# Conditioned attention on one core: another order of the Strassen products, new tables of PSUM banks, and an end in halves and pairs of heads

## The chip, the core and the metric

The kernel runs on one core of a Trainium2 chip. The time is the device time of one execution in microseconds (us); times of before and after are medians of several runs. TensorE does the matrix products and writes them to PSUM, which has eight banks of 128 x 512 f32. ScalarE (ACT in the profile), VectorE (DVE) read the banks; GpSimd (POOL) works in SBUF only here; SyncE (SP) issues most DMAs. All arithmetic but that of the row maxima's split is f32.

## The reference

Attention with 16 heads of 32 over 8 sequences of 512 tokens, with a condition added to Q and K and the input added at the end:

```python
Q = _split_heads(x @ Wq.T + bq)
K = _split_heads(x @ Wk.T + bk)
V = _split_heads(x @ Wv.T + bv)
tQ = _split_heads(tokens @ Wq.T + bq)
tK = _split_heads(tokens @ Wk.T + bk)
cQ = Q + tQ
cK = K + tK
scores = jnp.einsum('bhqd,bhkd->bhqk', cQ, cK) / jnp.sqrt(jnp.float32(HEAD_DIM))
attn = jax.nn.softmax(scores, axis=-1)
out = jnp.einsum('bhqk,bhkd->bhqd', attn, V)
return x + out.transpose(0, 2, 1, 3).reshape(B, S, D_MODEL)
```

Here x is (8, 512, 512), tokens are (8, 1, 512), the weights 512 x 512.

## The kernel before, in words

The work is cut into 32 tiles t: sequence b = t // 4 and group r = t % 4 of four heads. A group's four heads lie on the four blocks of 32 partitions, so four products with a depth of 32 run at the same time on TensorE.

**A stage.** The loop over t has four stages, one for each block kc of 128 keys. Each begins with `exponentials(t, kc)`: for each head, the transposed row maximum is put in its bank by a product with ones (L485), the transposed scores are added to it (L488), and ScalarE takes the exponential into SBUF (L500 and, for two banks at once, L502). Then `row_max` of a later tile computes scores for 128 queries (L417); VectorE takes the negated maximum of two banks at a time (L426), and `denominators` has ScalarE compute the exponentials once more, into a tile that nobody reads, for their sums (L443). What follows depends on the stage:

- first stage: x is transposed for a later sequence (L225), and Q of a later tile pair is projected;
- second: `weighted` multiplies the exponentials with V (L507), copied out by VectorE (L529);
- third: K is projected; in odd t also `output` of the tile before, which transposes (L539), divides (L553), adds the input (L564, POOL) and stores;
- fourth: `transpose_max` turns the maxima of the next tile (L469, copied by L475), and V is projected (L320); in even t `output` stands here.

`split_max` (L457 to L460, POOL) divides a maximum into three bf16 parts before its transposes.

**Projections.** A sequence's projection is made by Strassen-like block products, seven products M1 to M7 in place of eight, of 256 columns each; block sums of x and of the weights (`xc`, `wc`) are prepared by VectorE and POOL. `project_pair` does one pair of head groups in two parts. `first_products` (odd t for Q and K, even t for V) makes M1, M6, M7 and half of M2's depth; ScalarE copies M1 out (L359), and VectorE adds the rest (L368, L346 or L343, L371 or L365). `other_products` makes M4, M5, the other half of M2, and M3, and adds them in (L382, L383, L346). Each product with its two depth blocks is four passes on TensorE. Tiles of the first sequence are projected by plain products instead (L255 and L281).

**Order.** The order on TensorE, ScalarE, VectorE and POOL is the order of the program; nothing is moved by a scheduler. Waits come from the data and from PSUM. All PSUM is one tile of eight banks, and `TURNS` says for each stage which banks serve: places 0 to 3 are the banks of the exponentials (2 and 3 next to each other), which serve other work once they are read, and 4 to 7 those of the scores for the maxima. A bank can be written again when its last reader is done. Eight tables are used in turn in the loop, from the fourth on in the prologue, and five more near the end.

**The end.** From t = 28 on there is less to project. The weighted sums are made in two halves there (`first_half`, L693, and `second_half`, L699), and the maxima of the last tile in pairs of heads by `row_max_pair`. In the last tile no denominators are computed beforehand: the exponentials are summed (`acc`, L823 and L827) and multiplied by ones (L517).

Of the kernel before, what the change touches and what calls it, by code (L numbers as in the profile page):

```python
# [9 lines left out]
F32 = mybir.dt.float32  # L10
BF16 = mybir.dt.bfloat16
AF = mybir.ActivationFunctionType
ALU = mybir.AluOpType
# [4 lines left out]
def kernel(  # L18
# [33 lines left out]
    nc = tc.nc  # L52
# [26 lines left out]
        (0, 3, 6, 7, 1, 2, 4, 5),  # L79
        (7, 2, 0, 1, 3, 4, 5, 6),  # L80
        (0, 3, 1, 2, 4, 5, 6, 7),
        (2, 3, 4, 5, 6, 7, 0, 1),
        (7, 2, 5, 6, 0, 1, 3, 4),
        (5, 2, 0, 1, 3, 4, 6, 7),
        (2, 3, 0, 1, 4, 5, 6, 7),
        (0, 5, 3, 4, 6, 7, 1, 2),

        (2, 5, 6, 7, 0, 1, 3, 4),
        (2, 5, 0, 1, 3, 4, 6, 7),
        (2, 5, 3, 4, 6, 7, 0, 1),  # L90
        (2, 5, 6, 7, 0, 1, 3, 4),
        (2, 5, 0, 1, 3, 4, 6, 7),
# [221 lines left out]
    def product(n, b, u, i, pt, kcs=(0, 1)):  # L314

        for kc in kcs:
            w = block_of_w(n, i, u, kc)
            if n == "v":
                xb = block_of_x(b, i, kc, slice(u * P, (u + 1) * P))
                nc.tensor.matmul(pt, xb, w, start=(kc == kcs[0]), stop=(kc == kcs[-1]))  # L320
            else:
                xb = block_of_x(b, i, kc, slice(0, HS))
                nc.tensor.matmul(pt, w, xb, start=(kc == kcs[0]), stop=(kc == kcs[-1]))  # L323
# [24 lines left out]
    def first_products(n, b, u, dens, small, late):  # L348

        one_, two_ = (banks(1), banks(2)) if late else (banks(0), banks(3))
        c1, c12, c2, c22 = parts_of(n, b, u)
        m1 = c2[:, 0, :]
        product(n, b, u, 1, one_[:, :HS])
        if late:
            product(n, b, u, 2, one_[:, HS:], (0,))
        nc.scalar.copy(m1, one_[:, :HS])  # L359
        dens()  # L360
        small()
        product(n, b, u, 6, two_[:, :HS])
        product(n, b, u, 7, two_[:, HS:])
        if late:
            nc.vector.tensor_tensor(c1[:, 0, :], one_[:, HS:], m1, ALU.add)  # L365
        else:
            product(n, b, u, 2, one_[:, HS:], (0,))
        nc.vector.tensor_tensor(c12, two_[:, :HS], m1, ALU.add)  # L368
        plus(n, b, u, 1, c22, two_[:, HS:], c12)
        if not late:  # L370
            nc.vector.tensor_tensor(c1[:, 0, :], one_[:, HS:], m1, ALU.add)  # L371

    def other_products(n, b, u, dens, small, at):
# [5 lines left out]
        product(n, b, u, 2, two_[:, :HS], (1,))  # L379
# [26 lines left out]
    def row_max(t, qc):  # L406
        if t >= T:
            return
        open_max(t)
        for j in range(HG):  # L410
            row_scores(t, qc, j, banks(HG + j))
        for pr in range(NP):
            row_max_of(t, qc, pr, banks(HG + pr * 2, 2))
# [16 lines left out]
    def row_max_pair(t, qc, pr):  # L430

        open_max(t)
        for i in range(2):
            row_scores(t, qc, pr * 2 + i, banks(2 + i))
        row_max_of(t, qc, pr, banks(2, 2))
# [28 lines left out]
    def transpose_max(t, bank):  # L464
# [10 lines left out]
        nc.vector.tensor_copy(maxT[t], pt[:, :S])  # L475
# [84 lines left out]
    def finish(t):  # L560
        b, g = divmod(t, G)
        y = res.pop(t)
        last = nc.vector if t == T - 1 else nc.gpsimd
# [91 lines left out]
    project_qk(1, "q", banks(0))  # L655
# [15 lines left out]
    transpose_x(NS + 2, banks(2))  # L671
    project_qk(2, "k", banks(1))
# [4 lines left out]
    transpose_x(NS + 3, banks(0))  # L677
    project_qk(3, "q", banks(2))
# [28 lines left out]
    for t in range(T - 3):  # L707
# [6 lines left out]
        if r % 2:  # L714
            turn_x = lambda: transpose_x(t + NS + 3, banks(1), nc.vector.tensor_copy)
            project_pair("q", *qk_of, dens, turn_x, False)
        else:
            transpose_x(t + NS + 3, banks(0), nc.scalar.copy)
            if t:
                project_pair("q", *qk_of, dens, nothing, (1, 2))  # L720
            else:
                dens()
                project_qk(3, "k", banks(1))
# [18 lines left out]
        if r % 2:  # L742
            project_pair("k", *qk_of, dens, lambda: output(t - 1, banks(1)), False)
        elif t:
            project_pair("k", *qk_of, dens, nothing, (0, 2))
        else:
            dens()
            project_v(3, banks(2))
# [5 lines left out]
        denominators(t + 2, 0, [0])  # L754
        transpose_max(t + 1, banks(0))
        rest = lambda: denominators(t + 2, 0, [1])
        put_out = lambda: output(t - 1, banks(3)) if t else None
        if r % 2:
            project_pair("v", b + 1, r, rest, nothing, (1, 3))
        else:  # L760
            project_pair("v", b + 1, r, rest, put_out, True)
        if t == T - 4:
            first_half(t, banks(1))
# [27 lines left out]
    row_max(t + 2, 2)  # L791
    transpose_max(t + 1, banks(0))
    row_max_pair(t + 2, 1, 1)
# [6 lines left out]
    row_max(t + 1, 3)  # L800
    split_max(t + 1)
    second_half(t - 1, pd)

    exponentials(t, 1, (3, 4, 6, 7))
    times_v(t, 0, pv)
    output(t - 1, pd)
    exponentials(t, 2, (0, 1, 3, 4))
    times_v(t, 1, pv)
    transpose_max(t + 1, pd)
    exponentials(t, 3, (6, 7, 0, 1))  # L810
    times_v(t, 2, pv)
    exponentials(t + 1, 0, (3, 4, 6, 7))
# [3 lines left out]
    output(t, pd)  # L816
    t += 1
    exponentials(t, 1, (0, 1, 3, 4))
# [5 lines left out]
    exponentials(t, 2, (6, 7, 0, 1))  # L824
# [3 lines left out]
    exponentials(t, 3, (3, 4, 6, 7))  # L828
# [3 lines left out]
    times_v(t, 3, pv)  # L832
    den = stage.tile([P, NC, D], F32, tag="w", name="den")[:, 0, :]
    nc.scalar.copy(den, pd)
    leave(t, pv)
    untranspose(den, psum[:, 0, :])
    untranspose(oT[t], psum[:, 1, :])
    invert(t, psum[:, 0, :].rearrange("p (c h e) -> p c h e", c=NS, h=HG)[:, :, :, 0:1])
    divide(t, psum[:, 1, :])
    finish(t)  # L840
# [31 lines left out]
```

## Time and profile before

| what | us |
|---|---|
| median of 3 runs | 775.22 (773.84 to 775.51) |
| the profiled execution | 773.71 |
| its span in the profile | 771.9 |
| TensorE busy | 756.5 |
| ScalarE busy | 626.2 |
| VectorE busy | 528.7 |
| POOL busy | 124.5 |
| first L485 of t = 0 | 58.38 after the start |
| first L485 of t = 30 | 739.71 after the start |

A row of the timeline has the start, the time from the first to the last end of the instructions merged in it, the engine, the line, the operation, its tiles and shapes and, in brackets, the idle time before it and what ended that. An f32 product is two records, one for each pass. The ends of TensorE's records are modelled: a record of 256 columns shows 0.38 us while the next one starts much sooner, so the starts of successive rows say more than the busy time.

### The profile page before, as it was taken

To read this page: it belongs to the slowest core of one execution; us is meant where nothing else is said; L and a number is where in the kernel's file an instruction comes from. 1 tells how busy PE (TensorE), PEld (TensorE's weight loads), DVE (VectorE), ACT (ScalarE), POOL (GpSimd) and SP (SyncE) were. 2 spreads that over 40 slices of the span, in tenths; PEclk is the share of its full clock that TensorE was granted. 3 is DMA by queue.
4 is the path that set the end of the run, shared out by engine and by line. 5 is a ranking of instruction groups with operands and counts; after the bars stand their busy time and mean duration, and the time that the engine had idled before them with its cause. 6 is when DMAs were issued, how large, how long until landed. Compare 5 with 4: busy or idle time off the path is not lost.

```text
span 771.9 us, 14075 instructions
## 1 busy us (share of the span) xinstructions
PE 756.5 (98%) x5368; PEld 427.8 (55%) x5368; DVE 528.7 (68%) x719; ACT 626.2 (81%) x1452; POOL 124.5 (16%) x209
## 2 busy tenths in 40 slices
PE   8999999999999999999999999999999999999896
PEld 5443566555556655556655555665555565555332
DVE  4455677677677776677767776777766777667754
ACT  2447788888888888888888888888888888888864
POOL 0062011111011111111111101111110111110120
PEclk9999999999999999999999999999999999999999
DMA  9010011101111110111111011110101101010100
GB/s 314 17 39 28 14 42 42 28 16 42 42 42 42 32 40 15 42 42 42 42 25 45 14 43 42 42 42 12 45 2 28 29 28 29 1 44 12 48 22 28
DMA packets 41555, 29.76 MB, mean 39 GB/s; under 512 B 2824, under 2 KB 35592, under 8 KB 41488
## 3 DMA queue, kind: packets, MB, share of 16 engines
q1 hardware_dynamic: 40912, 27.81, 12.5%
q10 hardware_dynamic: 576, 1.05, 0.4%
q8 instruction: 42, 0.69, 0.4%
q14 instruction: 25, 0.20, 0.1%
HBM read 20.47 MB, written 8.39 MB: 37 GB/s over the span
## 4 chain that ended last, share of the span: by engine, by line
PE 95%; DVE 2%; ACT 1%; DMA 1%; issue 0%; SPq 0%; DVEq 0%; ACTq 0%
PE psum L323 23%; PE psum L507 15%; PE psum L488 14%; PE psum L417 14%; PE psum L320 12%; PE psum L485 6%; PE psum L255 4%; PE psum L225 2%; PE psum L539 2%; PE psum L281 2%; PE psum L469 1%; ACT e L500 1%; DVE nmax L426 1%; DMA x<-in_x_dram 1%; PE psum L180 1%; ACT e L502 0%
## 5 line engine op out<-in xcount | busy, mean ns | idle before, releaser
L426 DVE TENSOR_REDUCE nmax<-psum 128x2 f32<-128x1024 f32 x256 | 301.7, 1219 | 146.6 <-PE psum L417 145.8
L443 ACT ACTIVATE dead<-psum,nmax 128x512 f32<-128x512 f32 x496 | 335.1, 691 | 26.9 <-DVE nmax L426 26.9
L500 ACT ACTIVATE e<-psum 128x512 f32<-128x512 f32 x270 | 145.8, 595 | 88.8 <-PE psum L488 88.8
L417 PE MATMUL psum<-kT,qT 32*128 32x512 f32 x1024 | 140.9, 598 | 0.9 <-ACT e L502 0.9
L488 PE MATMUL psum<-qT,kT 32*128 32x512 f32 x1024 | 132.7, 588 | 0.0
L502 ACT ACTIVATE e<-psum 128x1024 f32<-128x1024 f32 x121 | 124.9, 1032 | 0.0
L507 PE MATMUL psum<-e,v 128*32 128x512 f32 x1024 | 118.6, 596 | 0.1
L443 ACT ACTIVATION_READ_ACCUMULATOR dead<-psum,nmax 128x1 f32 x496 | 103.6, 209 | 0.0
L457 POOL CAST split<-nmax 128x16 bf16<-128x16 f32 x32 | 8.1, 254 | 551.4 <-DVE nmax L426 551.4
L417 PEld LDWEIGHTS psum<-kT,qT 32*128 32x128 f32 x1024 | 67.5, 183 | 51.7 <-ACT dead L443 31.1
L507 PEld LDWEIGHTS psum<-e,v 128*32 128x32 f32 x1024 | 29.5, 109 | 82.4 <-issue 58.6
L485 PE MATMUL psum<-maxT,onesb 3*128 3x512 bf16 x512 | 51.8, 384 | 2.1 <-DVE res L553 0.8
L488 PEld LDWEIGHTS psum<-qT,kT 32*128 32x128 f32 x1024 | 51.1, 185 | 2.5
L564 POOL TENSOR_TENSOR res<-res,xr 128x512 f32<-128x512 f32 x31 | 39.4, 1272 | 74.0 <-DVE res L553 74.0
L485 PEld LDWEIGHTS <-onesb 3*128 3x128 bf16 x512 | 13.4, 91 | 64.8 <-issue 60.0
L529 DVE COPY oT<-psum 128x512 f32<-128x512 f32 x30 | 20.8, 692 | 39.7 <-PE psum L507 39.7
L323 PE MATMUL psum<-xc,wc_q 128*128 128x256 f32 x168 | 41.1, 380 | 0.2
L323 PE MATMUL psum<-xc,wc_k 128*128 128x256 f32 x168 | 40.9, 379 | 0.0
L320 PE MATMUL psum<-wc_v,xc 128*128 128x256 f32 x168 | 40.9, 379 | 0.0
L129 POOL TENSOR_TENSOR xr<-xr,bvb 128x512 f32<-128x512 f32 x32 | 40.5, 1268 | 0.0
L323 PEld LDWEIGHTS psum<-xc,wc_q 128*128 128x128 f32 x168 | 30.8, 190 | 4.6 <-ACT e L502 1.0
L320 PEld LDWEIGHTS psum<-wc_v,xc 128*128 128x128 f32 x168 | 30.9, 190 | 3.7
(135 smaller groups left out, 817.5 us busy)
## 6 DMA issues: line engine op xcount, KB each, us to landing
x<-in_x_dram SPq DMA_DIRECT2D x33, 256.0 KB, 2.7
xr<-in_x_dram SPq DMA_DIRECT2D x32, 256.0 KB, 3.1
out_dram<-res SPq DMA_DIRECT2D x32, 256.0 KB, 2.4
w_q<-in_L_cond_Wq_dram ACTq DMA_DIRECT2D x4, 256.0 KB, 4.4
w_k<-in_L_cond_Wk_dram SPq DMA_DIRECT2D x4, 256.0 KB, 5.0
w_v<-in_L_cond_Wv_dram SPq DMA_DIRECT2D x4, 256.0 KB, 6.0
bvb<-in_L_cond_bv_dram SPq DMA_DIRECT2D x1, 256.0 KB, 5.3
cond_sb<-in_cond_dram SPq DMA_DIRECT2D x1, 16.0 KB
```

The source lines that it names most:

```text
L129: nc.gpsimd.tensor_tensor(xr[t], xr[t], bias, ALU.add)
L320: nc.tensor.matmul(pt, xb, w, start=(kc == kcs[0]), stop=(kc == kcs[-1]))
L323: nc.tensor.matmul(pt, w, xb, start=(kc == kcs[0]), stop=(kc == kcs[-1]))
L417: nc.tensor.matmul(pt, qkT["q", t][r, qc * P : (qc + 1) * P], qkT["k", t][r, :], start=True, stop=True,)
L426: nc.vector.tensor_reduce(nmax[t][:, qc, pr * 2 : pr * 2 + 2, 0], pt, AX.X, ALU.max, negate=True)
L443: nc.scalar.activation(dead, banks(HG + j), AF.Exp, bias=nmax[t][:, qc, j, :], accum_out=sums[t][:, qc, j, :],)
L485: nc.tensor.matmul(bank[j], onesb[r, :], maxT[t][r, :], start=True, stop=False)
L488: nc.tensor.matmul(bank[j], qkT["k", t][r, kc * P : (kc + 1) * P], qkT["q", t][r, :], start=False, stop=True,)
L500: nc.scalar.activation(e[:, i, :], bank[pr * 2 + i], AF.Exp)
L502: nc.scalar.activation(e, banks(2, 2), AF.Exp)
L507: nc.tensor.matmul(pt[j * HD : (j + 1) * HD, :], vs[b % 2][:, kc, (g * HG + j) * HD : (g * HG + j + 1) * HD], es[t, kc, j // 2][:, j % 2, ...
L564: last.tensor_tensor(y, y, xr.pop(t), ALU.add)
```

## The change

1. `first_products` puts M6 and the half of M2 in one bank and M7, which now comes last, in the second half of M1's bank, for Q, K and V alike. `late` and its two forms are gone.
2. V's first half has all of M1 before the transposes of the maximum and, in even t, of the output; V's other half has M4 and M5 before the transposes (`small` is now called in `other_products` too). All four denominators stand behind the copy of M1, where two stood ahead.
3. Of K's M2, the half depth of the first part is made for 128 of the 256 columns. For the others POOL copies M1, and `other_products` makes both depth blocks.
4. New tables of banks, and other places in them for the work of the prologue and the loop.
5. In the fourth stage of t = 28 ScalarE copies the transposed maxima, the denominators come after that, and the output uses another bank.
6. The maxima of the last tile are spread over other stages in pairs of heads (`row_max_pairs`); t = 30 has its output behind the next exponentials, with the addition by VectorE; the last tile's output is copied, divided, added and stored in two halves.

```diff
     TURNS = [
-        (0, 3, 6, 7, 1, 2, 4, 5),
         (7, 2, 0, 1, 3, 4, 5, 6),
-        (0, 3, 1, 2, 4, 5, 6, 7),
-        (2, 3, 4, 5, 6, 7, 0, 1),
-        (7, 2, 5, 6, 0, 1, 3, 4),
-        (5, 2, 0, 1, 3, 4, 6, 7),
-        (2, 3, 0, 1, 4, 5, 6, 7),
-        (0, 5, 3, 4, 6, 7, 1, 2),
-
-        (2, 5, 6, 7, 0, 1, 3, 4),
-        (2, 5, 0, 1, 3, 4, 6, 7),
+        (7, 0, 3, 4, 5, 6, 1, 2),
+        (3, 0, 4, 5, 1, 2, 6, 7),
+        (2, 5, 0, 1, 6, 7, 3, 4),
+        (7, 0, 5, 6, 3, 4, 1, 2),
+        (3, 0, 4, 5, 1, 2, 6, 7),
+        (4, 5, 0, 1, 6, 7, 2, 3),
+        (5, 0, 6, 7, 1, 2, 3, 4),
+
+        (2, 5, 6, 7, 3, 4, 0, 1),
+        (2, 5, 3, 4, 0, 1, 6, 7),
+        (2, 5, 0, 1, 6, 7, 3, 4),
+        (2, 5, 6, 7, 3, 4, 0, 1),
         (2, 5, 3, 4, 6, 7, 0, 1),
-        (2, 5, 6, 7, 0, 1, 3, 4),
-        (2, 5, 0, 1, 3, 4, 6, 7),
     ]
...
-    def first_products(n, b, u, dens, small, late):
-        one_, two_ = (banks(1), banks(2)) if late else (banks(0), banks(3))
+    def first_products(n, b, u, dens, small, at):
+        one_, two_ = banks(0), banks(at)
         c1, c12, c2, c22 = parts_of(n, b, u)
         m1 = c2[:, 0, :]
         product(n, b, u, 1, one_[:, :HS])
-        if late:
-            product(n, b, u, 2, one_[:, HS:], (0,))
         nc.scalar.copy(m1, one_[:, :HS])
         dens()
         small()
         product(n, b, u, 6, two_[:, :HS])
-        product(n, b, u, 7, two_[:, HS:])
-        if late:
-            nc.vector.tensor_tensor(c1[:, 0, :], one_[:, HS:], m1, ALU.add)
-        else:
-            product(n, b, u, 2, one_[:, HS:], (0,))
+        w = P if n == "k" else HS
+        product(n, b, u, 2, two_[:, HS : HS + w], (0,), slice(0, w))
+        product(n, b, u, 7, one_[:, HS:])
         nc.vector.tensor_tensor(c12, two_[:, :HS], m1, ALU.add)
-        plus(n, b, u, 1, c22, two_[:, HS:], c12)
-        if not late:
-            nc.vector.tensor_tensor(c1[:, 0, :], one_[:, HS:], m1, ALU.add)
+        nc.vector.tensor_tensor(c1[:, 0, :w], two_[:, HS : HS + w], m1[:, :w], ALU.add)
+        if w < HS:
+            nc.gpsimd.tensor_copy(c1[:, 0, w:], m1[:, w:])
+        plus(n, b, u, 1, c22, one_[:, HS:], c12)
...
         product(n, b, u, 4, one_[:, :HS])
         product(n, b, u, 5, one_[:, HS:])
-        product(n, b, u, 2, two_[:, :HS], (1,))
+        small()
+        if n == "k":
+            product(n, b, u, 2, two_[:, :P], (1,), slice(0, P))
+            product(n, b, u, 2, two_[:, P:HS], (1, 0), slice(P, HS))
+        else:
+            product(n, b, u, 2, two_[:, :HS], (1,))
         product(n, b, u, 3, two_[:, HS:])
...
+    def row_max_pairs(t, of, late=()):
+        open_max(t)
+        for k, (qc, pr) in enumerate(of):
+            for i in range(2):
+                row_scores(t, qc, pr * 2 + i, banks(HG + k * 2 + i))
+        row_max_of(t, *of[0], banks(HG, 2))
+        for f in late:
+            f()
+        row_max_of(t, *of[1], banks(HG + 2, 2))
...
-            project_v(3, banks(2))
+            project_v(3, banks(0))
...
         row_max(t + 2, 0)
-        denominators(t + 2, 0, [0])
-        transpose_max(t + 1, banks(0))
-        rest = lambda: denominators(t + 2, 0, [1])
-        put_out = lambda: output(t - 1, banks(3)) if t else None
-        if r % 2:
-            project_pair("v", b + 1, r, rest, nothing, (1, 3))
-        else:
-            project_pair("v", b + 1, r, rest, put_out, True)
         if t == T - 4:
-            first_half(t, banks(1))
+            transpose_max(t + 1, banks(0), nc.scalar.copy)
+            denominators(t + 2, 0)
+            output(t - 1, banks(1))
+            first_half(t, banks(3))
+            break
+        dens = lambda: denominators(t + 2, 0)
+
+        def small():
+            transpose_max(t + 1, banks(1))
+            if t and r % 2 == 0:
+                output(t - 1, banks(2))
+
+        project_pair("v", b + 1, r, dens, small, (0, 2) if r % 2 else 3)
         advance()
...
     exponentials(t, 3)
-    row_max(t + 2, 2)
-    transpose_max(t + 1, banks(0))
-    row_max_pair(t + 2, 1, 1)
+    row_max_pairs(
+        t + 2, [(1, 1), (2, 0)], [lambda: transpose_max(t + 1, banks(0))]
+    )
...
     exponentials(t, 0)
-    row_max(t + 1, 3)
+    row_max_pairs(t + 1, [(2, 1), (3, 0)])
+    second_half(t - 1, pd)
+
+    exponentials(t, 1, (3, 4, 6, 7))
+    row_max_pair(t + 1, 3, 1, HG + 2)
     split_max(t + 1)
-    second_half(t - 1, pd)
-
-    exponentials(t, 1, (3, 4, 6, 7))
     times_v(t, 0, pv)
...
     invert(t, sums[t])
-    output(t, pd)
     t += 1
-    exponentials(t, 1, (0, 1, 3, 4))
+    exponentials(t, 1, (3, 4, 0, 1))
+    untranspose(oT[t - 1], pd)
+    divide(t - 1, pd)
     times_v(t, 0, pv)
...
     nc.scalar.copy(den, pd)
-    leave(t, pv)
-    untranspose(den, psum[:, 0, :])
-    untranspose(oT[t], psum[:, 1, :])
-    invert(t, psum[:, 0, :].rearrange("p (c h e) -> p c h e", c=NS, h=HG)[:, :, :, 0:1])
-    divide(t, psum[:, 1, :])
-    finish(t)
+    oT[t] = op.tile([P, S], F32, tag="oT", name=f"oT_{t}")
+    two = [slice(0, HS), slice(HS, S)]
+    nc.vector.tensor_copy(oT[t][:, two[0]], pv[:, two[0]])
+    nc.scalar.copy(oT[t][:, two[1]], pv[:, two[1]])
+    pi, po = psum[:, 3, :], [psum[:, 4, :], psum[:, 6, :]]
+    untranspose(den, pi)
...
+    for i in range(2):
+        cs = slice(i * 2, i * 2 + 2)
+        for qc in (i * 2, i * 2 + 1):
+            nc.tensor.transpose(
+                po[i][:, qc * P : (qc + 1) * P], oT[t][:, qc * P : (qc + 1) * P], ident
+            )
...
+        last = (nc.gpsimd, nc.vector)[i]
+        last.tensor_tensor(res[t][:, cs], res[t][:, cs], xr[t][:, cs], ALU.add)
+        (nc.sync, nc.scalar)[i].dma_start(
+            out[b].rearrange("(c p) d -> p c d", p=P)[:, cs, g * P : (g + 1) * P], res[t][:, cs]
+        )
```

## The prediction

> **What bounds the kernel now.** I read the page first (busy shares, clock, chain), then TensorE's timeline in the steady loop, in the first tile and at the end, then VectorE's timeline beside it. All names and lines are those of the kernel before; a "stage" runs from one L485 row to the next.
>
> ```profile
> PE 756.5 (98%) x5368; PEld 427.8 (55%) x5368; DVE 528.7 (68%) x719; ACT 626.2 (81%) x1452; POOL 124.5 (16%) x209
> ...
> PEclk9999999999999999999999999999999999999999
> ...
> PE 95%; DVE 2%; ACT 1%; DMA 1%; issue 0%; SPq 0%; DVEq 0%; ACTq 0%
> ```
>
> TensorE is busy for 98% at full clock and is 95% of the chain. No other engine's average can give time back; only TensorE's own work, and the short holes inside its "busy" rows, can. These show in the starts of successive rows:
>
> ```profile
> 277.85 1.02 PE L417 MATMUL psum<-kT,qT 32*128 32x512 f32 x8
> 278.81 1.13 PE L323 MATMUL psum<-xT,wT_k 128*128 128x256 f32 x4
> ...
> 283.55 1.11 PE L417 MATMUL psum<-kT,qT 32*128 32x512 f32 x8
> 284.59 0.40 PE L469 MATMUL psum<-identb,split 128*128 128x128 bf16 x4
> 284.88 1.13 PE L320 MATMUL psum<-wT_v,xc 128*128 128x256 f32 x4
> 285.85 1.03 PE L320 MATMUL psum<-wc_v,xc 128*128 128x256 f32 x4
> 286.72 0.59 PE L320 MATMUL psum<-wT_v,xT 128*128 128x256 f32 x2
> ```
>
> A record is one pass. Passes of 256 columns follow each other every 0.216 us (285.85 to 286.72: four in 0.87), four concurrent 512-column ones every 0.43. Two fixed costs stand out. A change between the 32-row groups and the full array costs 0.095 (277.85 to 278.81 is 0.96 for 0.86 of work), and the first full f32 pass after it 0.104 more (284.88 to 285.85 is 0.97 for 0.86). Those remain. Beyond them are waits: 283.55 to 284.59 is 1.04, 0.08 over the 0.96; and the four transposes of the maximum take 0.29 instead of 0.22, after which the product pays its 0.104. The eight stages of the pair t=9, 10 start at 265.31, 271.06, 276.76, 282.47, 288.11, 293.76, 299.38, 304.64 and the next pair at 310.73; this repeats to 0.01 us through the loop.
>
> ```profile
> 270.81 0.42 DVE L368 TENSOR_TENSOR qT<-psum,qT 128x256 f32<-128x256 f32 x1 [0.36 <-PE psum L323]
> 271.27 0.48 DVE L346 SCALAR_TENSOR_TENSOR qT<-psum,tok,qT 128x256 f32<-128x256 f32 x1
> 271.67 0.41 DVE L371 TENSOR_TENSOR qT<-psum,qT 128x256 f32<-128x256 f32 x1
> ```
>
> This is where the 0.08 comes from: three additions end a first half, and the last ends at 272.08, 1.02 into the next stage. Its bank is L417's fourth, due at 1.09, and the weight load before it needs 0.1.
>
> ```profile
> 54.18 0.39 PE L469 MATMUL psum<-identb,split 128*128 128x128 bf16 x4
> 54.40 0.60 PE L225 MATMUL psum<-ident,x 128*128 128x128 f32 x4
> 54.84 3.60 PE L255 MATMUL psum<-xT,wT_q 128*128 128x512 f32 x8
> ...
> 59.29 0.39 PE L485 MATMUL psum<-maxT,onesb 3*128 3x512 bf16 x3 [0.53 <-DVE qT L268]
> ...
> 74.37 3.70 PE L281 MATMUL psum<-wT_v,xT 128*128 128x512 f32 x8 [1.22 <-ACT e L502]
> ...
> 716.58 0.66 PE L539 MATMUL psum<-ident,oT 128*128 128x128 f32 x4 [0.80 <-ACT e L502]
> ...
> 739.71 0.40 PE L485 MATMUL psum<-maxT,onesb 3*128 3x512 bf16 x4 [0.54 <-DVE maxT L475]
> ...
> 755.05 0.66 PE L539 MATMUL psum<-ident,oT 128*128 128x128 f32 x4 [0.87 <-DVE oT L529]
> ...
> 768.64 0.37 SPq L565 DMA_DIRECT2D out_dram<-res  x1
> ```
>
> These are the waits that come once: two in tile 0, three at the end, and the last store.
>
> **The loop, stage by stage** (odd t does first halves, even t the others).
>
> *M6 and M2 in one bank, M7 last.* The first two additions now run during M7's 0.86 us and one remains: it should end about 0.7 into the next stage, not 1.02. In the new tables its bank is L417's fourth or an earlier finished one. So the stage after Q's first half falls from 5.70 to the 5.62 of its even twin (293.76 to 299.38): 14 x 0.08 = 1.1. The Q stage itself begins behind V's first half in the same way (266.40 to 267.40, 0.05 too long): 12 x 0.05 = 0.6; at t=25 and 27, with no x left to transpose, M6 waits for the pair of exponentials at 3.34 in both kernels.
>
> *A quarter of K's M2 moved.* 0.216 leaves each odd third stage and enters each even one: zero on TensorE, whose columns are the same. But four passes of 256 columns become eight of 128. The row: f32 transposes of 128 columns, each with its own weight load, come every 0.109 (54.40 to 54.84), and the load of an f32 product shows as 0.104 where nothing covers it, so it just fits under 0.109. The Trainium skill ("TensorE: Matmul & The Clock Gate", section "Back-to-back issue gap") speaks against the split: in a stream of loads and matmuls it has some 81 ns each at 128 columns where streaming alone would need 56, because the load has its own budget. By the row the split costs nothing; with the page's 25 ns on 8 passes x 14 pairs, an estimate of 2.8 us. Bounds: zero (no column is saved, so no gain) to the load wholly bare, 8 x 0.104 x 14 = 11.6. I take zero, by the nearer row. The longer even stage also takes off a wait: its last denominators (ending at 305.58 in the trace, 0.94 into the next) now land before L417. VectorE's addition shrinks to 128 columns. POOL gets a copy of 128 columns, between the 0.25 of a 16-column cast and the 1.27 of a 512-column addition. It queues behind split and the output's addition and delays the residual's bias by that much, read stages later; its own reader comes four stages later. POOL is 16% busy: zero, and at most its own length if that cover were gone.
>
> *V's halves begin with products.* In odd t the transposes of the maximum move behind M4 and M5. At 54.18 such transposes inside full-array work cost 0.22 with no restart; I add 0.05 for the f32 load that four 0.056 passes cannot cover. The stage becomes 2.04 (to the end of L417 and the change) + 0.97 + 0.86 + 0.27 + 0.43 + 0.86 + 0.10 = 5.54 instead of 5.64: 14 x 0.10 = 1.4. maxT is then copied at about 4.9, 0.6 before its use. In even t M1 comes first, then the transposes, ready at 3.24, then the output's transposes. These now go to the third exponential bank, which the pair releases at 3.34 (716.58 is 3.34 after its stage's start). So 3.34 + 0.49 + 2.26 = 6.09, and L417's wait for K's last addition (0.02 more) gives 6.11 against 6.08: 13 x 0.03 = 0.4 lost. What is late there is no longer L417 but the pair. Bounds for the moved transposes: at best 0.05 better in odd t, where the f32 load is covered after all; at worst both restarts come again in the middle, +0.2 on 27 stages. I stay near 54.18, the only row of the kind.
>
> **Tile 0.** L485 of its first stage no longer uses the bank of L268: 0.7, and 0.2 in the two holes behind it, so 6.98 becomes 6.07. project_v(3) goes to the first exponential bank, free at its turn: the 1.3 before 74.37. In the fourth stage M6 waits for the pair: +0.05. Together 2.1. A new wait, of the first burst's fourth bank on a weight transpose that ScalarE ends at 24.4, is hidden: TensorE waits there for ScalarE at 29.3 anyway.
>
> **The end.** *t=28, fourth stage*: the output's transposes use the second bank (free at 2.42), and the pair's wait then starts first_half at 3.34: 5.19 instead of 5.78, 0.59. ScalarE's copy of maxT (0.47 by the spacing after its x copy) makes its denominators late and costs the next L417 0.23. *t=29, fourth stage*: maxT follows one maximum instead of two and two score tiles leave: 4.99 becomes 3.86, 1.13; the score pair comes back at t=30, second stage, as 0.95 less an 0.3 wait and rounding: 0.57. *t=30's output behind t=31's exponentials*: the 0.87 and its restart go; L485's second half then waits 0.2 for ScalarE: 0.6. The sums acc follow ScalarE, 0.1 sooner. *Halves*: den and its transposes as before; VectorE's half copy (0.41), ScalarE's after it (same bank, 0.37), then divide and add by halves, the POOL one about 0.7. The last store starts near 768.05 of the old scale instead of 768.64: 0.6. The addition and store of t=30 move from POOL to VectorE, behind acc; SP gets them about 5 us later than today (757.88), still 5 before the end. Two queues carry the last 128 KB each; I give the transfer no gain. Together 0.36 + 0.56 + 0.6 + 0.1 + 0.6 = 2.2.
>
> **Sum.** 1.1 + 0.6 + 1.4 - 0.4 + 2.1 + 2.2 = 7.0, and 0.1 of rounding: 7.1 us. The profiled execution took 773.71 (span 771.9, 1.8 around it), so it would take 766.6; it lies 1.5 under the median of the three runs, 775.22. The forecast is made on the median: 775.2 - 7.1 = 768.1.
>
> **Rivals.**
> - *The split M2 is bound by weight loads (slower).* Place: eight 128-column passes of 14 K pairs. Price: up to 0.104 each, 11.6, so 775.2 - 7.1 + 11.6 = 779.7. It turns the sign above 7.1 / 112 = 63 ns a pass. For it: 0.104 against 0.109 is no margin. Against: the transposes keep 0.109.
> - *The transposes restart the array.* Moved into the middle they pay 0.095 and 0.104 again: 27 x 0.2 = 5.4 back, 773.5. For it: behind L469 today the 0.104 is paid. Against: 54.18.
> - *The waits only change their name.* L417 still waits for the last addition (1.7 lost) and the even fourth stage pays another restart behind the pair (1.3): 771.1. For it: the addition's margin is 0.3 only.
>
> **How the numbers follow.** Forecast 0.72, its own range 766.0 to 770.5; names changed 0.10; restart 0.11; loads 0.07. The range, 765.0 to 772.0, takes in the third rival and leaves out 0.18. This measurement can tell about 0.2%, 1.55 us. Faster: 0.72 + 0.10 + half of the restart = 0.88. Same: the other half, 0.05. Slower: 0.07.
>
> **What will show it.** Right: stages of an odd/even pair near 5.71, 5.62, 5.49, 5.54, 5.66, 5.62, 5.48, 6.11; no hole before 59.29 and 74.37; two final stores on two queues. Wrong: 128-column passes more than 0.11 apart; a product's first pass behind L469 at 0.32; L417 rows over 1.05; an even fourth stage over 6.15.

## The result, and the profile after

| what | before | after |
|---|---|---|
| median, us | 774.41 (773.63 to 775.51, 6 runs) | 768.11 (766.91 to 770.46, 6 runs) |
| ratio | | 0.9922 [0.9905, 0.9939] |
| the profiled execution | 773.71 | 767.80 |
| its span | 771.9 | 766.0 |

The changed kernel is 0.8% faster. The forecast of 768.1 was a gain of 7.1 from a median of 775.2; with more runs the median of before is 774.4, and the two medians lie 6.3 apart. That 768.1 and 768.11 agree so closely is luck: the base was 0.8 too high and the gain 0.8 too large. In the two profiles, counted from the first exponentials, the loop and the end take 713.55 and 707.59, a gain of 5.96. The stages of the loop that the prediction listed came out within 0.03 us of it; what is missing of 7.1 in this profile, 1.1, is about what one stage near the end lost by running partly at half clock.

Lines are now those of the kernel after. L498 begins a stage (before: L485) and L501 adds its scores; L419 computes the scores for the maxima (L417); L324 and L321 are products of Q, K and of V (L323, L320); L482 transposes a maximum (L469), L552 an output (L539); L364, L365 and L347 are a first half's additions. Two lines of the page first, busy shares and the chain:

```profile
PE 754.7 (99%) x5424; PEld 426.3 (56%) x5424; DVE 521.5 (68%) x720; ACT 627.1 (82%) x1454; POOL 127.3 (17%) x223
...
PE 96%; ACT 1%; DVE 1%; DMA 1%; issue 0%; SPq 0%; DVEq 0%
```

TensorE has 56 passes more than before and is busy 1.8 us less: the split M2 makes more passes of the same columns, and the holes hidden in long rows have gone. It still sets the end. Next TensorE's timeline in the loop. The first two rows are from the second stage of t=9. Then come the fourth stage of t=9, up to the start of t=10, and the end of the third and the fourth stage of t=10:

```profile
268.15 0.39 PE L498 MATMUL psum<-maxT,onesb 3*128 3x512 bf16 x4
...
269.24 1.02 PE L419 MATMUL psum<-kT,qT 32*128 32x512 f32 x8
...
279.26 0.40 PE L498 MATMUL psum<-maxT,onesb 3*128 3x512 bf16 x4
...
281.31 1.13 PE L321 MATMUL psum<-wT_v,xc 128*128 128x256 f32 x4
282.27 1.03 PE L321 MATMUL psum<-wc_v,xc 128*128 128x256 f32 x4
283.14 0.39 PE L482 MATMUL psum<-identb,split 128*128 128x128 bf16 x4
283.36 0.65 PE L321 MATMUL psum<-wT_v,xT 128*128 128x256 f32 x2
283.85 1.03 PE L321 MATMUL psum<-wc_v,xT 128*128 128x256 f32 x4
284.81 0.40 PE L498 MATMUL psum<-maxT,onesb 3*128 3x512 bf16 x4
...
299.95 0.83 PE L324 MATMUL psum<-xT,wT_k 128*128 128x128 f32 x6
300.62 1.03 PE L324 MATMUL psum<-xT,wc_k 128*128 128x256 f32 x4
301.58 0.40 PE L498 MATMUL psum<-maxT,onesb 3*128 3x512 bf16 x4
...
302.67 1.11 PE L419 MATMUL psum<-kT,qT 32*128 32x512 f32 x8
303.71 1.13 PE L321 MATMUL psum<-wT_v,xT 128*128 128x256 f32 x4
304.68 0.39 PE L482 MATMUL psum<-identb,split 128*128 128x128 bf16 x4
304.92 0.65 PE L552 MATMUL psum<-ident,oT 128*128 128x128 f32 x4
305.41 1.03 PE L321 MATMUL psum<-wc_v,xc 128*128 128x256 f32 x4
```

Four readings. L419 behind Q's first half takes 1.02, with no stretch. The transposes inside the products (283.14) cost 0.22 and the next two passes 0.49 instead of 0.43: no restart of the array, only the f32 load. Six passes of 128 columns take 0.67 (299.95 to 300.62), 0.11 each. And in the even stage L419 does stretch (302.67, 1.11), but L552 waits for the pair of exponentials anyway: 304.92 is 3.34 after 301.58.

VectorE's timeline shows why 269.24 has no stretch:

```profile
267.50 0.41 DVE L364 TENSOR_TENSOR qT<-psum,qT 128x256 f32<-128x256 f32 x1
267.83 0.41 DVE L365 TENSOR_TENSOR qT<-psum,qT 128x256 f32<-128x256 f32 x1
268.26 0.48 DVE L347 SCALAR_TENSOR_TENSOR qT<-psum,tok,qT 128x256 f32<-128x256 f32 x1
```

Two additions start ahead of the stage's end at 268.15, and the last ends 0.59 into the next stage. Before, the last ended 1.02 into it.

At the end of the kernel, all engines' timeline (POOL and DVE in the first two rows, then the queues of SP and ACT):

```profile
761.93 0.72 POOL L881 TENSOR_TENSOR res<-res,xr 128x256 f32<-128x256 f32 x1 [17.03 <-DVE res L874]
762.26 0.67 DVE L881 TENSOR_TENSOR res<-res,xr 128x256 f32<-128x256 f32 x1
762.68 0.37 SPq L882 DMA_DIRECT2D out_dram<-res  x1
762.96 0.41 ACTq L882 DMA_DIRECT2D out_dram<-res  x1
```

The last store of before was issued at 768.64. What did not come as forecast is one stage of t=29, in TensorE's timeline and in the busy time by stretches (columns: stretch, its length, busy time and instructions of PE, PEld, DVE, ACT and POOL, granted clock, DMA share, GB/s):

```profile
722.52 1.13 PE L419 MATMUL psum<-kT,qT 32*128 32x512 f32 x4 [0.33 <-ACT e L515]
724.45 0.40 PE L498 MATMUL psum<-maxT,onesb 3*128 3x512 bf16 x4 [0.81 <-DVE res L566]
...
725.82 1.96 PE L419 MATMUL psum<-kT,qT 32*128 32x512 f32 x8
727.71 2.36 PE L520 MATMUL psum<-e,v 128*32 128x512 f32 x16
```

```profile
719.00:724.00 5.00, 4.20 (x30) 1.82 (x28) 3.97 (x6) 4.53 (x11) 0.00 (x0) 1.00 0.00 0
724.00:728.00 4.00, 3.55 (x24) 1.49 (x27) 1.72 (x3) 3.44 (x9) 1.27 (x1) 0.65 0.29 78
```

L419 takes 1.96 for eight passes instead of 1.03. The clock record of this trace has half speed from 725.22 to 728.63, and this third stage of t=29 takes 6.51 instead of 5.26. The page's row of the clock, in slices of 19 us, shows nothing of it.

### The profile page after: what moved, and what is told of

The parts are those of the page before. It is cut to its first block, busy times and chain, and to the rows that moved or that the text cites. A ratio compares the mean times of both kernels' runs of the same rounds, so it can differ in the third digit from the quotient of the medians.

```text
span 766.0 us, 14203 instructions
## 1 busy us (share of the span) xinstructions
PE 754.7 (99%) x5424; PEld 426.3 (56%) x5424; DVE 521.5 (68%) x720; ACT 627.1 (82%) x1454; POOL 127.3 (17%) x223
## 4 chain that ended last, share of the span: by engine, by line
PE 96%; ACT 1%; DVE 1%; DMA 1%; issue 0%; SPq 0%; DVEq 0%
PE psum L324 23%; PE psum L520 15%; PE psum L501 14%; PE psum L419 14%; PE psum L321 12%; PE psum L498 6%; PE psum L255 4%; PE psum L225 2%; PE psum L552 2%; PE psum L281 2%; PE psum L482 1%; DMA x<-in_x_dram 1%; ACT e L513 1%; PE psum L180 1%; ACT e L515 0%
## 5 line engine op out<-in xcount | busy, mean ns | idle before, releaser
L419 PE MATMUL psum<-kT,qT 32*128 32x512 f32 x1024 | 138.9, 598 | 0.3 <-ACT e L515 0.3
L501 PE MATMUL psum<-qT,kT 32*128 32x512 f32 x1024 | 132.7, 589 | 0.0
L419 PEld LDWEIGHTS psum<-kT,qT 32*128 32x128 f32 x1024 | 64.7, 183 | 52.0 <-issue 27.7
L498 PE MATMUL psum<-maxT,onesb 3*128 3x512 bf16 x512 | 51.2, 384 | 1.7 <-DVE res L566 0.8
L501 PEld LDWEIGHTS psum<-qT,kT 32*128 32x128 f32 x1024 | 51.1, 185 | 2.5 <-issue 0.2
L498 PEld LDWEIGHTS <-onesb 3*128 3x128 bf16 x512 | 13.3, 91 | 63.6 <-issue 54.1
L324 PE MATMUL psum<-xc,wc_q 128*128 128x256 f32 x168 | 43.4, 380 | 0.3 <-ACT e L515 0.3
L321 PE MATMUL psum<-wc_v,xc 128*128 128x256 f32 x168 | 43.2, 380 | 0.0
L324 PE MATMUL psum<-xc,wc_k 128*128 128x256 f32 x168 | 43.2, 380 | 0.0
L324 PEld LDWEIGHTS psum<-xT,wT_k 128*128 128x128 f32 x168 | 26.4, 190 | 12.8 <-ACT e L513 10.6
L324 PEld LDWEIGHTS psum<-xc,wc_q 128*128 128x128 f32 x168 | 30.8, 190 | 4.7 <-ACT e L515 1.1
```

Source lines behind the costliest of these rows:

```text
L419: nc.tensor.matmul(pt, qkT["q", t][r, qc * P : (qc + 1) * P], qkT["k", t][r, :], start=True, stop=True,)
L498: nc.tensor.matmul(bank[j], onesb[r, :], maxT[t][r, :], start=True, stop=False)
L501: nc.tensor.matmul(bank[j], qkT["k", t][r, kc * P : (kc + 1) * P], qkT["q", t][r, :], start=False, stop=True,)
```

## The experiments

In the tables "from the first exponentials" is the time from the first L498 row of t=0 to the end of the profile. It leaves out the start of the kernel, which moved that row between 58.4 and 61.3 us from profile to profile.

### The changed kernel once more

No edit.

> The changed kernel as it is. Its profile has one stretch of 3.41 us at half clock (725.22 to 728.63), in which the third stage of t=29 takes 6.51 us where the prediction's sum has 5.26. Theory: the clock is decided at fixed intervals of 3.41 us that do not start with the kernel, and the two holes of the second stage (0.4 and 0.8 us) fell into one interval there; with another phase the stage takes 5.26, the span is 764.8, and all other stages repeat to 0.02 us. Rival: the new end always brings the drop, so the stage is 6.5 again and the span 766.0.

Measured: 767.37 (766.96 to 767.83), ratio 0.991 [0.9895, 0.9924]. Full clock throughout, and the third stage of t=29 is back at 5.255; all other stages are as in the first profile to 0.01, except the fourth of t=29 (3.86 for 3.80). The two rows that stand where the clock had halved:

```profile
725.07 0.40 PE L498 MATMUL psum<-maxT,onesb 3*128 3x512 bf16 x4 [0.81 <-DVE res L566]
...
726.15 1.18 PE L419 MATMUL psum<-kT,qT 32*128 32x512 f32 x8
```

The same hole of 0.81 stands in front, and the clock holds. So the half-clock stretch belongs to the execution, not to the instructions alone.

### M7 beside M6, and M2 last

```diff
-        product(n, b, u, 2, two_[:, HS : HS + w], (0,), slice(0, w))
-        product(n, b, u, 7, one_[:, HS:])
+        product(n, b, u, 7, two_[:, HS:])
+        product(n, b, u, 2, one_[:, HS : HS + w], (0,), slice(0, w))
```

The addition of M7 stands ahead of that of M2 to match.

> The new tables kept, but in the first halves M7 goes with M6 and the half of M2 comes last in M1's bank, as before. Theory (the order counts: two additions are left behind the last pass and end 1.0 us into the next stage): the second stage of odd t goes from 5.62 back to about 5.70, the first from 5.70 to about 5.76 where V's first half precedes; the fourth of odd t stays near 5.54, since K's addition has only 128 columns. Together 14 x 0.08 + 12 x 0.06 = 1.9 us more. Rival (the new tables alone removed the wait): no stage changes by more than 0.01.

Measured: 771.02 (770.6 to 772.21), ratio 0.9959 [0.9944, 0.9974]. Odd tiles: 5.72, 5.70, 5.49, 5.70. The second stage is back at its old 5.70. The first went only to 5.72, not to the 5.76 expected, and the fourth has grown by 0.16, which I had not expected. TensorE's weight loads and VectorE name the cause, around 281 us in this kernel's timeline:

```profile
281.60 0.49 PEld L419 LDWEIGHTS psum<-kT,qT 32*128 32x128 f32 x8 [0.53 <-DVE kT L347]
```

```profile
280.60 0.42 DVE L364 TENSOR_TENSOR kT<-psum,kT 128x256 f32<-128x256 f32 x1 [0.31 <-PE psum L324]
281.06 0.48 DVE L347 SCALAR_TENSOR_TENSOR kT<-psum,tok,kT 128x256 f32<-128x256 f32 x1
```

With M7 in M6's bank the first addition begins only when M7 is written, 5.45 after the stage's start (275.15); in the changed kernel it begins 5.05 after it. K's M2 is now only 0.22 of work behind which to hide two additions, so L347 ends 0.9 into the next stage and L419 waits for it. The sum over an odd tile is 0.018 + 0.081 - 0.003 + 0.158 = 0.25, by 14 tiles 3.6; from the first exponentials the profile has 710.2 for 706.4, 0.3 of it a single pause (the third stage of t=17). So the order, with the sharing of banks that goes with it, gives the second stage's gain; of the first stages' 0.6 it gives 0.2. The new tables alone do not: with them and the other order half of the change's gain is gone.

### K's M2 whole

```diff
-        w = P if n == "k" else HS
+        w = HS
```

The other half computes M2 from its second block alone, for K as for V and Q.

> All 256 columns of K's M2 have their first depth block in the first half again, and POOL copies nothing. Theory (the quarter is worth nothing, a 128-column pass takes 0.112 us): the third stages go from 5.50 and 5.50 to 5.71 and 5.26; the even fourth stage stays within 0.03 of 6.09, because its later wait for the pair hides what L417 loses to the late denominators; the whole changes by less than 0.5 us. Rival (the longer even stage takes a wait off the fourth): that stage becomes 6.18 or more, 1.3 us more in all.

Measured: 767.7 (766.68 to 769.59), ratio 0.9916 [0.9896, 0.9937]. The odd third stage takes 5.704 instead of 5.496, the even one 5.264 instead of 5.503: an odd and an even tile together 0.03 less. The quarter moved is worth nothing; it costs 0.4 over 14 pairs. Its profile had half clock from 726.74 to 730.15, in the third stage of t=29 again (6.53). It also has a pause that the changed kernel does not have: the second stage of t=16 takes 5.950 instead of 5.617. The two profiles of the combined kernel below, which has K's M2 whole too, have the same pause in the same stage, so as built this edit nets only about 0.1.

### The places where TensorE waited at t=29, filled

```diff
     row_max_pair(t + 2, 0, 0)
+    fill(t, 1, banks(1))
     advance()
...
     row_max_pair(t + 2, 0, 1)
+    fill(t, 3, banks(1))
     advance()
...
         t + 2, [(1, 1), (2, 0)], [lambda: transpose_max(t + 1, banks(0))]
     )
+    fill(t, 3, banks(1))
```

`fill(t, n, pt)` is n products of the maxima, 512 columns of bf16 each, into a bank that is overwritten afterwards.

> Products of ones with the transposed maxima, whose result nobody reads, are added in the holes before the next stage in the first (1), second (3) and fourth stage (3) of t=29; the output is unchanged. Theory (an interval with little work on TensorE halves the clock): no half-clock stretch before the last product, third stage of t=29 at 5.26, the other three within 0.1 of what they are, span about 764.8. Rival (the drop has another cause, or the added products come in the way): a half-clock stretch is there again, or stages of t=29 grow by more than 0.2.

Measured: 766.99 (766.79 to 767.53), ratio 0.9906 [0.9889, 0.9922]. Full clock up to 762.66; t=29 takes 5.604, 5.187, 5.259 and 3.858. The first stage grew by 0.13, a little over the 0.1 allowed, and the second shrank by 0.07, so the filling itself gains nothing at full clock (706.5 from the first exponentials, 706.4 without it). What it does to the clock is weighed below over all profiles.

### V's transposes ahead of M4 and M5, in the bank as it stands

```diff
+        if n == "v":
+            small()
         product(n, b, u, 4, one_[:, :HS])
         product(n, b, u, 5, one_[:, HS:])
-        small()
+        if n != "v":
+            small()
```

> The changed kernel with one step undone: in the fourth stage of odd t the four transposes of the maximum come ahead of V's M4 and M5 again, behind the denominators, as before the change. My theory: a product after those transposes pays the f32 load of 0.104 behind the change of 0.095, and the transposes themselves take 0.07 more than 0.22 behind the change, so this stage goes from 5.544 back to 5.62 to 5.64 and all other stages stay within 0.02: 14 x 0.09 = 1.3 us longer than the changed kernel, about 768.7 on the scale where that one took 767.4. Rival (the new tables brought this gain, the order brought nothing): the stage stays at 5.54 and the time at 767.4.

Measured: 772.65 (771.99 to 774.37), ratio 0.9964 [0.9952, 0.9976]. The odd fourth stage takes 5.811, not 5.63. The kernel's timeline, at t=9, tells why (L485 is the transposes' line here):

```profile
285.58 0.38 PE L485 MATMUL psum<-identb,split 128*128 128x128 bf16 x4 [0.30 <-ACT e L516]
```

The transposes' bank is read by the second exponential, and that early in the stage ScalarE still has it. This kernel tested the bank along with the order, so both explanations missed and the order stayed open.

### The same with the two exponential banks exchanged

```diff
-        (5, 0, 6, 7, 1, 2, 3, 4),
+        (0, 5, 6, 7, 1, 2, 3, 4),
...
-            transpose_max(t + 1, banks(1))
+            transpose_max(t + 1, banks(1 - r % 2))
...
-        project_pair("v", b + 1, r, dens, small, (0, 2) if r % 2 else 3)
+        project_pair("v", b + 1, r, dens, small, (1, 2) if r % 2 else 3)
```

> The transposes of the maximum ahead of M4 and M5 once more in the fourth stage of odd t, this time with the first two exponential banks exchanged in that stage's row of the table, so that the transposes take the bank of the first exponential and M4 and M5 that of the second (in the first try the transposes took the second's bank and waited 0.30 for ScalarE, and the stage took 5.811). My theory: without that wait the order alone remains, the restart behind 0.056 passes: 5.62 to 5.64 against the changed kernel's 5.544, 14 x 0.09 = 1.3 us longer than it, and the next stages within 0.02 of the changed kernel's. Rival (what the order costs is only the wait for the bank): the stage falls to 5.55 and nothing is lost.

Measured: 769.8 (769.75 to 770.49), ratio 0.9925 [0.99, 0.995]. The odd fourth stage takes 5.641, what it took before the change. The rows of that stage, the transposes in L485:

```profile
283.17 0.40 PE L485 MATMUL psum<-identb,split 128*128 128x128 bf16 x4
283.54 1.13 PE L321 MATMUL psum<-wT_v,xc 128*128 128x256 f32 x4
284.51 1.03 PE L321 MATMUL psum<-wc_v,xc 128*128 128x256 f32 x4
```

No wait, but 0.37 from the transposes to the product (0.22 inside the products) and then 0.97 for 0.86 of work. That is the order's whole effect: 0.097 by 14, 1.4. The exchanged row did one thing more, which I had not thought of: the last product ahead of tile 0 uses the same row of the table, and the first stage of t=0 took 6.976 instead of 6.067.

```profile
59.92 0.39 PE L501 MATMUL psum<-maxT,onesb 3*128 3x512 bf16 x2 [0.52 <-DVE qT L268]
```

This is the wait for L268 that before had at 59.29, back with its bank: 0.91, the size forecast for tile 0's first stage. Together 2.3; the profile has 709.0 for 706.4 from the first exponentials, 0.3 of it a single pause.

### V's last product of tile 0 in a bank of the pair

```diff
-            project_v(3, banks(0))
+            project_v(3, banks(2))
```

> The changed kernel with V's third unfactored product of tile 0 put back into a bank of the exponentials' pair. My theory: the third stage of t=0 goes from 5.68 to 6.97 because the product waits for ScalarE's pair, and nothing else moves: 1.3 us longer, about 768.7 beside 767.4. Rival (in the new tables the pair is read sooner, or the next stage takes the wait up): under 0.3 us.

Measured: 772.47 (770.39 to 773.91), ratio 0.9954 [0.9939, 0.997].

```profile
74.91 3.70 PE L281 MATMUL psum<-wT_v,xT 128*128 128x512 f32 x8 [1.22 <-ACT e L515]
```

The third stage of t=0 takes 6.969 for 5.677: 1.29, as expected. The profile has more: half clock at t=29 (third stage 6.85, 1.6 more), and, against the expectation that nothing else moves, a pause of 0.29 to 0.31 in the fourth stage of t=4, 8, 12, 16, 20 and 24, 1.75 in all. The three add up to the whole difference (711.05 for 706.41 from the first exponentials). VectorE and TensorE at the start of such a stage, here t=8, and below them the same stage of the changed kernel:

```profile
259.85 0.75 DVE L347 SCALAR_TENSOR_TENSOR kT<-psum,tok,kT 128x512 f32<-128x512 f32 x1 [0.55 <-PE psum L324]
260.75 1.14 PE L419 MATMUL psum<-kT,qT 32*128 32x512 f32 x8 [0.15 <-DVE kT L347]
```

```profile
256.53 0.75 DVE L347 SCALAR_TENSOR_TENSOR kT<-psum,tok,kT 128x512 f32<-128x512 f32 x1 [0.20 <-PE psum L324]
257.45 1.11 PE L419 MATMUL psum<-kT,qT 32*128 32x512 f32 x8
```

The stages start at 259.34 and 256.36, so the same addition begins 0.51 and 0.17 after the start, and L419 has to wait for the late one. The last section comes back to these pauses.

### The end as it was

The loop and tile 0 of the changed kernel; from the fourth stage of t=29 the code of the kernel before, with the banks renamed to the new tables.

> The changed kernel up to the third stage of t=29 (its loop, its tables, tile 0, and the fourth stage of t=28 as changed), and from there the end as it was: two maxima before the last transposes of a maximum, no score pair moved, t=30's output ahead of t=31's second exponentials, one whole last output with one store. My theory, by the stages of the two traces: t=29 fourth 3.86 becomes 4.99 (+1.13), t=30 second 3.63 becomes 3.06 (-0.57), t=31 first two 5.28 become 6.10 (+0.82), and the last store is issued about 0.6 later with about 0.2 more behind it: 2.2 us longer, about 769.6 beside 767.4. Rival (only t=29's stage counts, because the work moved is paid for later): 0.6 us or less.

Measured: 770.29 (768.83 to 772.53), ratio 0.994 [0.992, 0.9959]. From the first exponentials 708.5 for 706.4, 2.1. By stages: t=29 fourth 4.99 (+1.13), t=30 second 3.06 (-0.57), t=31's first three 8.50 for 7.46 (+1.03), and from there to the end 11.70 for 11.23 (+0.47). The wait that the change removed is back at t=31:

```profile
751.18 0.66 PE L552 MATMUL psum<-ident,oT 128*128 128x128 f32 x4 [0.87 <-DVE oT L542]
```

### The pieces that paid, together

K's M2 whole, the places filled, and in even fourth stages the output first:

```diff
         def small():
-            transpose_max(t + 1, banks(1))
             if t and r % 2 == 0:
-                output(t - 1, banks(2))
+                output(t - 1, banks(1))
+                transpose_max(t + 1, banks(2))
+            else:
+                transpose_max(t + 1, banks(1))
```

> The changed kernel with three edits: K's M2 whole in both halves (no quarter moved, no copy on GpSimd), dummy products of the maxima (7 passes, results not used) in the three places of t=28 and t=29 where TensorE waited, and in the fourth stage of even t the output's transposes ahead of those of the maximum, each in the other's bank. My theory: 0.03 x 14 = 0.4 from the whole M2 as measured, about 0.4 from the filled places plus no half-clock stretch of 1.25, and 6.086 to about 6.06 in the even fourth stage, 13 x 0.025 = 0.3, because the output no longer waits for the exponentials' pair: 766.2 to 766.4, 0.991 of the changed kernel's 767.4 less 0.002, that is a ratio to the kernel before of about 0.990. Rival (output first makes the copy of the maximum late for the next stage's exponentials, 0.1 or more in each of 13 stages): 767.5 or more.

Measured: 766.76 (766.37 to 769.53), ratio 0.9903 [0.9885, 0.9921]. The even fourth stage takes 6.066 instead of 6.086, 0.02 and not 0.025. Then once more beside the changed kernel on one chip:

> The version with K's M2 whole, filled places at t=28 and 29 and the output ahead of the transposed maximum in even fourth stages, beside the changed kernel on the same chip. By the stages of its first profile (odd/even pair 45.17 instead of 45.22, even fourth 6.066) it is 0.6 us shorter than the changed kernel, 0.0008 of it, and 1.2 more in executions where the changed kernel has the half-clock stretch: ratio 0.9895 to 0.9905 to the kernel before. Rival (the gain lies within what the start of the loop varies by, 58.4 to 61.3 us in the profiles so far): the two medians agree within 0.3 us or turn round.

> The changed kernel itself once more, as the comparison on this chip: 767.3 to 768.2 and a ratio of 0.991 to 0.992; the third stage of t=29 at 5.26 or, with a half-clock stretch, at 6.5; all other stages as in its first two profiles.

Measured: 766.78 (766.55 to 768.94), ratio 0.9888 [0.9867, 0.9908], and for the changed kernel 768.48 (767.04 to 770.49), 0.9904 [0.9884, 0.9924]. By stages the combined kernel is shorter by 0.4 + 0.3 - 0.1 = 0.6, and about 0.35 of that is lost to the pause at t=16, which both of its profiles have: 706.1 from the first exponentials in each, for 706.4. The changed kernel's profile had half clock once more, third stage of t=29 6.56. The medians point the way the stages do, but the two intervals overlap: a gain of 0.3 us is shown by the profiles, not by the times.

## The half clock, over thirteen profiles

In every clock record the stretches between changes, apart from the first and last cut off by the record, last a multiple of 3.413 us, among them 3.413 at half clock, 37.547 (11 of them), 720.21 (211), 761.17 (223). So the boundaries can be continued through each trace from its first one. The Trainium skill ("TensorE: Matmul & The Clock Gate", section "What's actually happening") says the same: an activity window of 3413 ns that runs free of the kernel. The table takes, around t=29's third stage, the interval of least work: where it ends, the share of its 3.413 us in which TensorE streamed, and the stage's time. That share is my sum: 0.84 ns for a column of an f32 pass (0.216 for 256), half of that for bf16, passes that overlap counted once.

| kernel | end of the interval, us from the start of t=29's third stage | streamed share | third stage, us |
|---|---|---|---|
| V's last product in a bank of the pair | 0.00 | 0.499 | 6.85 |
| changed kernel, third profile | 0.56 | 0.526 | 6.56 |
| K's M2 whole | 0.60 | 0.534 | 6.53 |
| V's transposes first | 0.72 | 0.543 | 6.51 |
| changed kernel, first profile | 0.77 | 0.543 | 6.51 |
| changed kernel, second profile | -0.18 | 0.550 | 5.26 |
| M2 last | 1.20 | 0.606 | 5.26 |
| old end | 1.29 | 0.633 | 5.26 |
| before | 2.12 | 0.715 | 5.26 |
| V's transposes first, banks exchanged | 2.52 | 0.714 | 5.25 |
| filled | 0.22 | 0.668 | 5.26 |
| combined, first | -0.78 | 0.720 | 5.26 |
| combined, second | -0.63 | 0.719 | 5.25 |

All five with a share up to 0.543 lost the clock for the next 3.413 us, all eight from 0.550 on kept it, and no other interval at full clock between 54 and 758 us of any of these profiles has less than 0.55. Outside that stretch the same share draws no such line. Full-clock intervals with less kept the clock near the end of the kernel (0.42, ending at 762.4, in the second profile of the changed kernel; 0.43 at 764.4 in the old end; 0.49 at 762.8 in the first profile of the changed kernel; 0.51 at 769.3 with V's transposes first) and once at the start (0.51 at 8.1, second profile of the changed kernel). So the border between 0.543 and 0.550 belongs to this place, and what the clock counts stays open. The filled kernel had its boundary at 0.22, among those that lost it, and kept the clock, with 0.668, in the one profile there is. So at t=29 the stretch comes when one fixed interval holds both holes, of 0.33 and 0.81 us, with little streaming around them, and it costs 1.25 to 1.3 (1.6 once). The same skill page advises against idle gaps of some 3.4 us (section "HAM oscillation — how this bites in real kernels"); here two holes of 1.14 together were enough, and the measurement decides.

Before has nearly the same two holes (0.35 and 0.80). Its one profile, with the boundary at 2.12, kept the clock; whether it loses the same time in other executions, and how often beside after, is not shown.

## Why the prediction was right

The mechanism was right: the waits named went, at close to the sizes given. In part the sum's agreement is luck: the quarter of K's M2 lost 0.4 that was put at nothing, and V's even halves and the end came out 0.3 and 0.2 better than forecast.

The sum of 7.1 against the second profile of the changed kernel, which has full clock, counted from the first exponentials (before 713.55, after 706.41: 7.14):

| step | forecast | measured |
|---|---|---|
| M7 last, second stages of odd t | 1.1 | 79.77 - 78.63 = 1.14 |
| M7 last, first stages of odd t | 0.6 | 80.45 - 79.84 = 0.61 |
| quarter of K's M2 moved | 0 | 2.91 - 3.35 = -0.44 |
| V begins with products, odd t | 1.4 | 78.98 - 77.62 = 1.36 |
| V's even halves | -0.4 | 79.05 - 79.11 = -0.06 |
| tile 0 | 2.1 | 25.27 - 23.13 = 2.14 |
| the end | 2.2 | 2.36 |

- **M7 last.** Right in size, and for the second stages shown by the kernel with M2 last, where they went back to 5.70. Of the 0.6 in the first stages that kernel lost only 0.2; which part of the change gives the rest was not tried. The last addition ended 0.59 into the stage; I had 0.7.
- **The split M2.** Passes of 128 columns came 0.109 to 0.112 apart, as the row of the transposes had said, and the estimate of 2.8 us from the skill's figure did not come. I took zero; the term was mis-sized by the 0.03 per pair that the smaller passes cost, 0.4. The first rival, loads that bind, is out: 0.112 is far from the 0.17 (0.109 and 0.063) at which it would have turned the sign.
- **V's transposes inside the products.** The pass after them took 0.27, the 0.05 added to 0.22, and the stage 5.54. The kernel with the exchanged banks gave 5.641 back. The second rival, a restart in the middle, is out.
- **The even fourth stage** took 6.086, not 6.11. The mis-sized term is L419's wait for K's last addition: I added 0.02 for it to a stage that already waited for the pair, while the row shows L552 3.34 after the stage's start in any case. The output first, ahead of the pair, takes 0.02 off.
- **Tile 0.** Both waits have gone at their sizes, 0.91 and 1.29, and each came back with its bank. The fourth stage cost the 0.05 forecast.
- **The end.** t=28's fourth stage gained 0.59 and the next lost 0.28 (0.23 forecast); t=29's fourth gained 1.13, t=30's second lost 0.57. Two terms were mis-sized. t=31's first three stages gained 1.03, not 0.6 + 0.1. In the first two (0.82) the wait for ScalarE is 0.11 by the rows (L501 to L552 takes 1.07 for 0.96), not 0.2, which gives half of what they gained beyond 0.6; the other half I cannot place. The third gained 0.21, not 0.1. The last part gained 0.47, not 0.6, and not where forecast. The last store is issued 8.17 after the start of t=31's fourth stage instead of 8.42, only 0.25 sooner, mostly because VectorE's half addition took 0.67 beside POOL's 0.72 and not the 0.41 of other halves. The other 0.22 lie behind the issue, where two stores of 128 KB stand in place of one of 256 KB and I had given the transfer no gain.
- **The third rival**, waits that only change their name (771.1), is out: no odd stage of the loop has a stretched L419, and the one in the even stage is hidden.
- **What the sum had no term for** is the half clock: 1.25 to 1.3 in two of three profiles of the changed kernel and as much or more in three of its variants, none forecast. My page reading took the "9" of the clock row for full clock everywhere, which slices of 19 us cannot show. The three pairs of medians lie 6.3 to 6.9 apart and not 7.1; how much of that is the half clock, and how much the start of the kernel, the runs do not separate.

## What to carry to other kernels

When TensorE is the bound, look at what its next bank waits for, and put last the product whose addition is the only one left, so that the others run under it; then put short transposes between full-array products rather than at a border where the array restarts. Moving work by quarters to even out two stages gave nothing where TensorE streamed through both anyway. Before small holes near the end are called harmless, add up how many of them can fall into one 3.4 us interval.

## What the runs showed that I had not expected

- At t=29, two holes of 0.33 and 0.81 us within one fixed interval of 3.413 us halved TensorE's clock for the next one, at a streamed share of 0.499 to 0.543; a share of 0.550 there did not, and at the start and the end of the kernel neither did shares of 0.42 to 0.51.
- Pauses of 0.29 to 0.35 us in one stage of an otherwise regular loop: six in the kernel with V's last product in a bank of the pair, and one each in five other profiles, at t=17 (M2 last) and at t=16 (banks exchanged, and all three with K's M2 whole). They go with the program: those three have it in the same stage, and none of the three profiles of the changed kernel has one. In all eleven the first late instruction is VectorE's, 0.51 to 0.56 into its stage instead of 0.16 to 0.20, and it stands at the same place in VectorE's order, its semaphore instructions counted: number 192, 320, 448, 576, 704 and 832 in the kernel with six, 576 in each of the others, always 64 more than a multiple of 128. A DMA packet of 8192 bytes of the kind "instruction" starts 0.7 to 1.0 us later each time. With V's last product in a bank of the pair VectorE has one instruction fewer, so the addition L347 moves into that place; in the changed kernel a semaphore instruction stands there. That loading VectorE's program in blocks of 128 instructions makes the delay fits all this, but no run moved VectorE's program alone, so it is argued and not shown.
- The start varies more than several of these edits: the first exponentials came between 58.4 and 61.3 us. In the two profiles with the latest start (60.9 and 61.3) the clock record has 3.413 us of half clock at 9.1 and 8.1 us.
